# Block products in a graph-network kernel: sums kept in three PSUM banks with a read between the products, and SBUF sums taken off GpSimd

## The chip, the core and the metric

The kernel runs on one core of one Trainium2 chip. The metric is the device time of one execution in microseconds (us). Three executions took 2376.56, 2377.87 and 2381.8 us, so the median is 2377.87 us. In what follows PE is TensorE, DVE is VectorE, ACT is ScalarE, POOL is GpSimd and SP is SyncE.

## What is computed

The input is 128 graphs of 64 nodes with 256 features, and one 64 x 64 adjacency matrix for each. Four layers follow each other, each of them `x = layernorm(x + layer(x, adj))`, all in float32. Cut to what matters:

```python
# layer 0: five steps of a gated recurrent cell
for l in range(5):
    agg = A^T @ (h @ weight[l])
    r = sigmoid(agg @ Wir + h @ Whr + b);  z = sigmoid(agg @ Wiz + h @ Whz + b)
    n = tanh(agg @ Win + bi + r * (h @ Whn + bh))
    h = (1 - z) * n + z * h
# layer 1: (adj @ x) @ W1 -> RMS norm -> silu -> @ W2        (256 -> 1024 -> 256)
# layer 2: log map, adj @ x, exp map, projection onto a ball  (row by row)
# layer 3: attention with exp(e_i + f_j) weighted by adj
```

The five recurrent steps hold most of the work: each one multiplies a 256-feature state and a 256-feature aggregate by six 256 x 256 weight blocks.

## The kernel before

Two graphs fill the 128 partitions, four such pairs make a group of R = 512 columns, and 16 groups (g = 0 to 15) make the batch. `group(g)` (from L611) records all operations of one group as a stream. Nothing is issued while recording: `Flow.either` (L150) keeps, for every operation, the engine or the choice of two engines, an assumed duration, and what it must wait for. `Plan.advance` (L71) then lays the operations of up to four groups (WINDOW) out on the engines, earliest start first, with the rank of each 4 us stretch taken from the string CHOICES. The order so found is fixed on every engine by `Flow.issue`. So a change of one operation, of the rank functions or of CHOICES can move every instruction of the program. The planner also knows that a POOL sum and a DVE operation marked `port` shall not run at the same time; nothing on the chip enforces that order between the two engines.

Three recording helpers matter here. `copied` (L330) and `scaled` (L335) are reads of a PSUM bank that go to ACT or DVE (on DVE with a handicap of 0.4 us, LATER). `summing` (L344) is a sum of two SBUF tiles that goes to DVE or, with a handicap of 1.5 us, to POOL; all such sums have the line L347 in the profile. `dve` and `pool` go to one engine.

Every large matrix product is cut into 2 x 2 blocks and done with seven block products instead of eight, from sums of the inputs (tiles tA, tB, ts, s, made by `summing`) and sums of the weights (made once). With m11, m12, ms1 to ms4 and mn22 for the products and u = m11 + ms2, the four result blocks are

```
m11 + m12      u + ms1 + ms4      u + ms3 + mn22      u + ms3 + ms1
```

- The gates r and z (`gate`, L776, and `plus`, L831): banks p1, pu, pv, pw (shown as p_r, p_u, p_v, p_w). m11 is copied out of p1 (`copied`), then m12 is added to it in the bank and ACT takes the tanh straight from there. The other three blocks are built in SBUF tiles uu and uz by five `plus` sums on DVE, each of which reads one bank of 128 x 512.
- The state's share of n (`state_side`, L795, banks p_hx, p_hy): one copy, one scaled read, two plain sums (L793) and three sums with bias (L807).
- The input's share of n (`input_side`, L843, banks p_ix, p_iy): six sums on DVE (L852), four of 256 columns, one that adds one product to three blocks (768) and one that reads two products at once (512).
- The hidden layer of layer 1 (`by_sums`, L956, banks p_1h, p_uh, p_vh, p_wh): for each of two column halves q, two copies and five sums (L972). Its squares are added up by seven `summing` calls (L949 to L955, tile sqt).
- The way back (`by_sums_back`, L1022, banks p_ox, p_oy): seven sums of 256 columns (L1051) and one of 512 (L1067).

A bank is one unit for the planner and for the semaphores: a product into a bank waits for every earlier read of that bank. In one recurrent step of one group, nine products are recorded behind such a read of their own bank (three in the gates, four in the state's share, two in the input's share).

The last two groups (14 and 15) have `summed` false: their layer norms take their statistics on DVE.

Of the kernel before, what the change touches and what calls it, by code (L numbers as in the profile page):

```python
# [16 lines left out]
P = 128  # L17
# [36 lines left out]
class Plan:  # L54
# [15 lines left out]
    def advance(self, until, rank):  # L70
# [3 lines left out]
        while self.left and clock["PE"] < until:  # L74
            best = None
            for s in range(self.first, min(self.first + flow.WINDOW, len(self.queues))):
                for e, q in self.queues[s].items():
                    opened = False
                    for _, o in zip(range(flow.AHEAD[e]), q):
# [12 lines left out]
                        key = (t + flow.LATER.get((e, len(o.ways) > 1 and o.eng), 0.0), *rank(s, o))  # L92
# [36 lines left out]
class Flow:  # L129
# [16 lines left out]
    LATER = {("DVE", "ACT"): 0.4, ("POOL", "DVE"): 1.5}  # L146
# [6 lines left out]
    WINDOW, STRETCH, LAGS = 4, 4.0, (60.0,)  # L153
    CHOICES = ("0011200000220021202000222000000001000001011000200022110000002002022002112211120201000120000200002022"
               "0200011101200002210100000000222211100211000102210222210000000000211100011010001021111120212101000000"
               "0010210010100101002201011100000000000021002211102210200001020200200202200000012002201221010100002000"
               "0202022000000020022202222010022000002022022002222202220200110100022000000220200020002220011010102100"
               "2200000002202000002001110222000022000000000000022210200012222220120100201112002012121100100100121001"
               "201010010201111111011011000100111011111111111110110111000111011101100001010000100100")
# [81 lines left out]
def kernel(  # L241
# [102 lines left out]
    def summing(n, o, x0, x1, op, w, r):  # L344

        def run(v):
            return lambda: v.tensor_tensor(o(), x0(), x1(), op)  # L347
        flow.either([("DVE", 0.145 + 0.00105 * n, run(nc.vector)), ("POOL", 0.24 + 0.00211 * n, run(nc.gpsimd))], w, r, port=("DVE", "POOL"))
# [264 lines left out]
    def group(g):  # L613
# [128 lines left out]
        def gated(l, h):  # L742
# [49 lines left out]
            def onto(o, ps, j, x, w, r):  # L792
                dve(HR + 44, lambda: nc.vector.tensor_add(o(), ps[:, j * HR:(j + 1) * HR], x()), w, [ps, *r])  # L793

            def state_side():  # L795

                px, py = bank("p_hx"), bank("p_hy")
                su, sv = ((lambda c=c: uz[:, c, half(0)]) for c in range(2))

                def b(c):  # L800
                    return half_b[:, 2 * KD + c:2 * KD + c + 1]

                def out(n, c):
                    return lambda: hnb[:, c, half(n)]

                def biased(n, c, ps, j, x, r):
                    dve(HR + 44, lambda: nc.vector.scalar_tensor_tensor(  # L807
                        out(n, c)(), ps[:, j * HR:(j + 1) * HR], b(c), x(), OP.add, OP.add), [(hnb, (n, c))], [ps, r, half_b])

                prod(px, 0, w_hn, m11, block(0, 0)[1], True)  # L810
                copied(HR, su, lambda: px[:, :HR], [(uz, (0, 0))], [px])
                prod(px, 0, w_hn, m12, block(1, 0)[1])
                scaled(HR, out(0, 0), lambda: px[:, :HR], lambda: 1.0, lambda: b(0), [(hnb, (0, 0))], [px, half_b])
                prod(px, 1, w_hn, ms2, sum_of(t2)[1])
                onto(su, px, 1, su, [(uz, (0, 0))], [(uz, (0, 0))])
                prod(py, 0, w_hn, ms3, sum_of(t3)[1], True)
                onto(sv, py, 0, su, [(uz, (0, 1))], [(uz, (0, 0))])
                prod(py, 1, w_hn, ms1, sum_of(t1)[1])
                prod(py, 0, w_hn, mn22, sum_of(t4)[1])
                biased(0, 1, py, 0, su, (uz, (0, 0)))  # L820
                biased(1, 1, py, 1, sv, (uz, (0, 1)))
                prod(py, 1, w_hn, ms4, block(1, 1)[1])
                biased(1, 0, py, 1, su, (uz, (0, 0)))

            p1, pu, pv, pw = bank("p_r0"), bank("p_u"), bank("p_v"), bank("p_w")
# [5 lines left out]
            def plus(o, n, ps, x, m):  # L831
                dve(R, lambda: nc.vector.tensor_add(o[:, :, half(n)], feats(ps.tile()), x[:, :, half(m)]), of(o, n), [ps, *of(x, m)])  # L832
# [10 lines left out]
            def input_side():  # L843
# [3 lines left out]
                def quarters():  # L847
                    return uu.tile().rearrange("p c (n r) -> p (c n) r", n=2)

                def onto(i, n, src, ps):  # L850
                    w = [(uu, (j % 2, j // 2)) for j in range(i, i + n)]
                    dve(HR * n + 40, lambda: nc.vector.tensor_add(  # L852
                        quarters()[:, i:i + n, :], src(), quarters()[:, i:i + n, :]), w, [ps, *w])

                prod(px, 0, w_in[l], m11, block(0, 0)[0], True)
                prod(px, 1, w_in[l], m12, block(1, 0)[0])
                onto(0, 1, lambda: px[:, :HR].unsqueeze(1), px)
                onto(0, 1, lambda: px[:, HR:2 * HR].unsqueeze(1), px)
                prod(py, 1, w_in[l], ms3, sum_of(t3)[0], True)
                prod(py, 0, w_in[l], ms1, sum_of(t1)[0])  # L860
                onto(3, 1, lambda: py[:, HR:2 * HR].unsqueeze(1), py)
                onto(3, 1, lambda: py[:, :HR].unsqueeze(1), py)
                prod(px, 0, w_in[l], ms2, sum_of(t2)[0])
                onto(1, 3, lambda: over(px[:, :HR], 3), px)
# [356 lines left out]
```

## Time and profile before

One execution was profiled: it took 2377.02 us, of which the span from the first to the last instruction is 2375.1 us.

| | before |
|---|---|
| median of three runs | 2377.87 us |
| profiled execution / its span | 2377.02 / 2375.1 us |
| PE busy, matmul instructions | 2317.0 us (98%), 12754 |
| DVE busy | 1988.6 us (84%) |
| ACT busy | 1272.5 us (54%) |
| POOL busy | 378.6 us (16%) |
| chain that ended last | PE 88%, DVE 9%, ACT 2% |
| DMA | 35.3 MB, mean 15 GB/s |

How to read it: a float32 matmul of 256 columns is two instructions of 128 x 256, each shown as 379 ns long, but they follow each other every 216 ns, since they are pipelined. A short wait of PE is therefore inside its busy time, and waits are better read from the starts of its instructions. PE's weight loads have a row of their own, PEld. An idle time is named with the instruction that ended it. In the groups of instructions, the last number after the bar is the idle time of the engine just before them.

### The profile page before, as it was taken

The numbers are of one execution on the slowest core, as the hardware profiler recorded it, in microseconds if no ns is written. First come the engines' busy times: TensorE is split into PE (matmuls) and PEld (weight loads), VectorE is DVE, ScalarE is ACT, GpSimd is POOL, SyncE is SP. The second block draws the span as 40 slices with busy tenths as digits, with TensorE's granted clock in tenths as the row PEclk, the third lists the DMA queues.
The fourth block names the chain that finished last, engine by engine and source line by source line (L and its number), as shares of the span: only waits on it lengthen the run. The fifth ranks groups of instructions, "written<-read, shape, count | busy, mean of one in ns | idle before, by whom it ended". The sixth has DMA issues, their size and how long they took to land.

```text
span 2375.1 us, 34664 instructions
## 1 busy us (share of the span) xinstructions
PE 2317.0 (98%) x12754; PEld 2056.6 (87%) x12754; DVE 1988.6 (84%) x4305; ACT 1272.5 (54%) x2793; POOL 378.6 (16%) x343
## 2 busy tenths in 40 slices
PE   9999999999999999999999999999999999999985
PEld 7888988898888888888898888988889889888874
DVE  5788888888888888888888888888888888789896
ACT  3344564756555556565555556555555544635475
POOL 3200101110130110112011110202211101001141
PEclk9999999999999999999999999999999999999987
DMA  3000000000000000000000000000000000000000
GB/s 123 10 1 12 1 27 3 27 3 1 29 1 19 12 1 30 1 30 1 27 3 1 30 1 30 1 11 19 1 30 1 27 3 1 19 10 1 18 10 18
DMA packets 40520, 35.29 MB, mean 15 GB/s; under 512 B 9972, under 2 KB 39696, under 8 KB 40352
## 3 DMA queue, kind: packets, MB, share of 16 engines
q1 hardware_dynamic: 38624, 31.20, 4.2%
q8 instruction: 101, 1.65, 0.3%
q10 hardware_dynamic: 1328, 1.31, 0.2%
q0 software_dynamic: 400, 0.57, 0.1%
q14 instruction: 67, 0.55, 0.1%
HBM read 24.69 MB, written 8.39 MB: 14 GB/s over the span
## 4 chain that ended last, share of the span: by engine, by line
PE 88%; DVE 9%; ACT 2%; issue 1%; POOL 1%; POOLq 0%; ACTq 0%; DVEq 0%
PE p_w L782 11%; PE p_v L782 11%; PE p_r L782 11%; PE ps_agg L315 7%; PE p_hy L788 6%; PE p_iy L788 5%; PE p_u L782 5%; PE p_oy L1042 5%; PE p_hx L788 4%; PE p_ix L788 4%; PE p_ox L1042 4%; PE ps_hr L656 3%; PE p_vh L967 2%; PE p_1h L967 2%; PE p_wh L967 2%; PE ps_a L315 2%
## 5 line engine op out<-in xcount | busy, mean ns | idle before, releaser
L712 POOL TENSOR_TENSOR rstd<-ve,pow 128x4 f32<-128x4 f32 (+1 forms) x64 | 77.5, 1212 | 801.2 <-DVE ve L704 761.0
L782 PE MATMUL p_v<-tA,w_h 128*128 128x256 f32 x640 | 170.4, 379 | 0.1
L782 PE MATMUL p_v<-tB,w_a 128*128 128x256 f32 x640 | 169.2, 379 | 0.5 <-DVE tB L347 0.5
L782 PE MATMUL p_r<-hT,w_h 128*128 128x256 f32 x640 | 168.5, 380 | 0.0
L782 PE MATMUL p_r<-agg,w_a 128*128 128x256 f32 x640 | 166.6, 379 | 0.7 <-ACT agg L333 0.7
L333 ACT COPY agg<-ps_agg 128x512 f32<-128x512 f32 x156 | 91.1, 584 | 121.8 <-PE ps_agg L315 121.1
L835 ACT ACTIVATE U<-U,half_b 128x512 f32<-128x512 f32 (+1 forms) x160 | 94.1, 629 | 108.1 <-DVE U L832 108.0
L315 PEld LDWEIGHTS ps_agg<-edge,hr 128*128 128x128 f32 x1024 | 137.3, 191 | 7.5 <-ACT hr L333 0.2
L315 PE MATMUL ps_agg<-edge,hr 128*128 128x128 f32 x1024 | 139.0, 275 | 0.0
L788 PE MATMUL p_hy<-tA,w_hn 128*128 128x256 f32 x480 | 132.8, 381 | 3.6 <-DVE V L793 2.3
L788 PE MATMUL p_iy<-tB,w_in 128*128 128x256 f32 x480 | 133.4, 380 | 1.4 <-DVE V L852 1.4
L782 PEld LDWEIGHTS p_v<-tB,w_a 128*128 128x128 f32 x640 | 120.2, 190 | 16.5 <-DVE tB L347 0.9
L782 PEld LDWEIGHTS p_r<-agg,w_a 128*128 128x128 f32 x640 | 119.6, 190 | 16.4 <-ACT agg L333 1.1
L782 PEld LDWEIGHTS p_v<-tA,w_h 128*128 128x128 f32 x640 | 119.2, 190 | 15.9 <-DVE V L832 0.5
L835 ACT ACTIVATE V<-V,half_b 128x256 f32<-128x256 f32 (+1 forms) x160 | 87.5, 586 | 79.8 <-DVE V L832 79.7
L782 PEld LDWEIGHTS p_r<-hT,w_h 128*128 128x128 f32 x640 | 115.4, 190 | 13.1 <-issue 0.5
L333 ACT COPY hr<-ps_hr 128x512 f32<-128x512 f32 x117 | 68.2, 585 | 103.5 <-PE ps_hr L656 94.8
L899 ACT ACTIVATE V<-V,cols 128x512 f32<-128x512 f32 x96 | 64.7, 715 | 104.0 <-DVE V L852 103.9
L338 ACT ACTIVATE x_n<-y,off,rstd 128x256 f32<-128x256 f32 x175 | 92.3, 589 | 46.3 <-DVE off L716 46.2
L701 ACT ACTIVATE x_n<-y,mv 128x256 f32<-128x256 f32 x168 | 83.3, 498 | 57.0 <-DVE mv L699 57.0
L656 PE MATMUL ps_hr<-ident,hT 128*128 128x128 f32 x640 | 101.4, 273 | 6.8 <-DVE hT L907 6.5
L656 PEld LDWEIGHTS ps_hr<-ident,hT 128*128 128x128 f32 x640 | 79.7, 141 | 25.9 <-issue 9.9
(292 smaller groups left out, 6327.8 us busy)
## 6 DMA issues: line engine op xcount, KB each, us to landing
x<-in_x_dram SPq DMA_DIRECT2D x16, 512.0 KB, 3.9
xr<-in_x_dram SPq DMA_DIRECT2D x16, 512.0 KB, 3.9
out_dram<-x_n SPq DMA_DIRECT2D x16, 512.0 KB, 2.9
edge<-in_adj_dram SPq DMA_DIRECT2D x32, 64.0 KB, 2.3
wm<-in_L_gnn_weight_dram SPq DMA_DIRECT2D x5, 256.0 KB, 5.1
w2f<-in_L_gnn_W_dram SPq DMA_DIRECT2D x4, 256.0 KB, 6.2
w_in_L_gnn_w_hh_dram<-in_L_gnn_w_hh_dram ACTq DMA_DIRECT2D x1, 512.0 KB, 5.3
w_in_L_gnn_w_ih_dram<-in_L_gnn_w_ih_dram ACTq DMA_DIRECT2D x1, 512.0 KB, 6.7
```

The lines of the kernel that those rows point to most:

```text
L315: return nc.tensor.matmul(o, lhsT, rhs, start=(k == 0), stop=(k == nk - 1))
L333: flow.either([("ACT", 0.22 + 0.00077 * n, lambda: nc.scalar.copy(o(), i())), ("DVE", 0.145 + 0.00105 * n, lambda: nc.vector.tensor_copy(o ...
L338: flow.either([("ACT", 0.3 + 0.0008 * n, lambda: nc.scalar.activation(o(), i(), AF.Identity, bias=bias(), scale=scale())), ("DVE", 0.145 + ...
L656: turn(lambda j=j, c=c: nc.tensor.transpose(ps[:, j * D + c * P:j * D + (c + 1) * P], src[:, c, (HB * n + j) * P:(HB * n + j + 1) * P], id ...
L701: act(400, lambda b=b: nc.scalar.activation(o[:, b, :], y[:, b, :], AF.Square, bias=mv[:, b, 0:1], accum_out=st[:, b, 1:2]), [(o, b), (st, ...
L712: pool(1.25, lambda: nc.gpsimd.tensor_tensor(rstd[:, :m, :], ve[:, :m, :], pow2[:, :m, :NB], OP.pow), [rstd], [ve])
L782: pe(HR, lambda i=i, w=w, c=c: nc.tensor.matmul(ps[:, c * HR:(c + 1) * HR], w[:, m, c * P:(c + 1) * P], v[i][0](), start=first and i == 1 ...
L788: pe(HR, lambda: nc.tensor.matmul(ps[:, j * HR:(j + 1) * HR], w[:, m, :], v[0](), start=first, stop=True, skip_group_check=True), [ps], [( ...
L835: act(HR if len(w) == 1 else R, lambda: nc.scalar.activation(o(), src(), AF.Tanh, bias=half_b[:, i * KD + c:i * KD + c + 1], scale=0.5), w ...
L899: act(R, lambda c=c: nc.scalar.activation(uu[:, c, :], uu[:, c, :], AF.Tanh, bias=bih(2 * KD + c)), [*of(uu, 0, c), *of(uu, 1, c)], [*of(u ...
L967: pe(HR, lambda c=c: nc.tensor.matmul(ps[:, c * HR:(c + 1) * HR], w1f[:, w, (2 * q + c) * P:(2 * q + c + 1) * P], v[0](), start=first and ...
L1042: pe(128, lambda j=j, k=k: nc.tensor.matmul(ps[:, i * HR + j * P:i * HR + (j + 1) * P], val(v[k // 2])[:, k % 2, j * P:(j + 1) * P], w2f[: ...
```

## The change

The seven products are gathered in three banks, and the sums that share u are taken from one bank that keeps growing. For the gates, bank pa receives m11, ms2, ms1 and ms4 one after the other and is read after each; pb receives m12; pc receives ms3 and then mn22. The first reads of a block become copies (`taken`, ACT or DVE) and only the second reads are sums on DVE. The last read of pa is ACT's tanh itself.

```diff
+            gate(pa, m11, block(0, 0), True, True)
+            taken(uu, 0, pa)
+            gate(pb, m12, block(1, 0), True, True)
+            plus(uu, 0, pb)
+            tanh_r(0)
...
-            gate(pu, ms2, sum_of(t2), True, True)
-            plus(uu, 1, pu, uu, 1)
-            gate(pv, ms3, sum_of(t3), True, False)
-            plus(uz, 1, pv, uu, 1)
-            gate(pw, ms1, sum_of(t1), True, False)
-            gate(pv, mn22, sum_of(t4), False, True)
-            plus(uz, 1, pw, uz, 1)
-            plus(uz, 0, pv, uu, 1)
-            gate(pw, ms4, block(1, 1), False, True)
-            plus(uu, 1, pw, uu, 1)
+            gate(pa, ms2, sum_of(t2), False, True)
+            taken(uz, 0, pa)
+            gate(pc, ms3, sum_of(t3), True, True)
+            taken(uz, 1, pc)
+            gate(pa, ms1, sum_of(t1), False, True)
+            plus(uz, 1, pa)
+            gate(pc, mn22, sum_of(t4), False, True)
+            plus(uz, 0, pc)
+            gate(pa, ms4, block(1, 1), False, True)
+            tanh_r(1, pa)
```

`state_side` follows the same pattern in regions of two banks: four reads with bias (`begun`, a `scaled`, ACT or DVE) and three sums (`added`) in place of a copy, a scaled read, two sums and three sums with bias. Behind a read of their own bank stand now four products in the gates, five in the state's share and five in the input's share.

```diff
+                def begun(n, c, ps, j):
+                    b = half_b[:, 2 * KD + c:2 * KD + c + 1]
+                    scaled(HR, lambda: hnb[:, c, half(n)], lambda: region(ps, j), lambda: 1.0, lambda: b, [(hnb, (n, c))], [ps, half_b])
+                def added(n, c, ps, j):
+                    dve(HR + 44, lambda: nc.vector.tensor_add(hnb[:, c, half(n)], region(ps, j), hnb[:, c, half(n)]),
...
                 prod(px, 0, w_in[l], m11, block(0, 0)[0], True)
+                prod(py, 0, w_in[l], m12, block(1, 0)[0], True)
+                onto(0, 0, px, 0)
+                prod(py, 1, w_in[l], ms3, sum_of(t3)[0])
+                onto(0, 0, py, 0)
                 prod(px, 0, w_in[l], ms2, sum_of(t2)[0])
+                onto(1, 1, py, 1)
+                onto(0, 1, px, 0)
                 prod(py, 1, w_in[l], mn22, sum_of(t4)[0])
+                prod(px, 0, w_in[l], ms1, sum_of(t1)[0])
+                onto(0, 1, py, 1)
+                onto(1, 1, px, 0)
+                prod(px, 0, w_in[l], ms4, block(1, 1)[0])
+                onto(1, 0, px, 0)
```

`input_side` (above) has seven sums of 256 columns in place of the six wider and narrower ones. `by_sums` has four copies and three sums for each half in place of two and five, and `by_sums_back` seven sums of 256 columns with the 512-column one gone.

The sums of SBUF tiles no longer have a choice of engines:

```diff
     def summing(n, o, x0, x1, op, w, r):
-
-        def run(v):
-            return lambda: v.tensor_tensor(o(), x0(), x1(), op)
-        flow.either([("DVE", 0.145 + 0.00105 * n, run(nc.vector)), ("POOL", 0.24 + 0.00211 * n, run(nc.gpsimd))], w, r, port=("DVE", "POOL"))
+        dve(n, lambda: nc.vector.tensor_tensor(o(), x0(), x1(), op), w, r, True)
+
+    def pool_sum(n, o, x0, x1, op, w, r):
+        pool(0.24 + 0.00211 * n, lambda: nc.gpsimd.tensor_tensor(o(), x0(), x1(), op), w, r)
```

`pool_sum` is used for x1 + b2 (tile xb, 128 x 1024) in all groups, and for the sums of squares (sqt, 128 x 512) and x3 + W_b (x_n, 128 x 1024) in groups 0 to 13. All other SBUF sums are DVE's.

The planner's order is written anew: LATER becomes SOONER (a handicap of 0.4 us for the DVE way of any operation with two ways), LAGS grows from one value to three (30, 90 and 150), which gives CHOICES the digits 0 to 4, and the string CHOICES is another one.

## The prediction, made before the changed kernel ran

> **What bounds the kernel now.** I read the page's busy shares first, then busy time by 100 us stretches, then who PE waits for.
>
> ```profile
> span 2375.1 us, 34664 instructions
> PE 2317.0 (98%) x12754; PEld 2056.6 (87%) x12754; DVE 1988.6 (84%) x4305; ACT 1272.5 (54%) x2793; POOL 378.6 (16%) x343
> ```
>
> ```profile
> 1000.00:1100.00 100.00, 98.51 (x549) 87.35 (x548) 86.82 (x194) 60.81 (x132) 15.21 (x13) 1.00 0.06 18
> ...
> 2200.00:2300.00 100.00, 88.58 (x484) 76.54 (x482) 86.13 (x194) 56.50 (x121) 27.23 (x21) 0.96 0.04 12
> 2300.00:2375.00 75.00, 50.08 (x301) 43.63 (x300) 53.25 (x189) 41.72 (x95) 19.39 (x15) 0.80 0.06 22
> ```
>
> The columns are stretch, length, then PE, PEld, DVE, ACT and POOL busy, then the granted clock. PE is full at clock 1.00 until 2200; the last 175 us are a tail with holes and a lower clock.
>
> Busy time hides short PE waits, so I made a ledger from the starts of its instructions. At the median step of each size (216 ns at 256 columns, 111 at 128, and so on) the 12754 matmuls need 2286.6 us. Before the first lie 2.5 us and behind the last start 11.5. The remaining 74.7 are stalls: 33.5 before 2200 (25.1 in 36 stalls over 0.15 us, 9.6 in stalls of 0.02 to 0.15, the rest rounding) and 41.2 in the tail. The change has the same matmuls, 6922 by the program's count in both orders; only the stalls can change.
>
> What makes the stalls? PE's waits name DVE mostly:
>
> ```profile
> PE ps_sup L315 <- ACT tan L1110: 10.8, 3, 9.5
> PE ps_hr L656 <- DVE hT L907: 6.5, 8, 1.3
> PE ps_T L646 <- ACT x_n L338: 5.4, 3, 2.6
> ```
>
> and the timeline shows what is behind the second line, DVE first, then POOL, then PE (start, duration, what):
>
> ```profile
> 1323.58 0.69 DVE L907 SCALAR_TENSOR_TENSOR hT<-hT,V 128x512 f32<-128x512 f32 x1
> 1324.19 1.76 DVE L347 TENSOR_TENSOR hT<-hT,V 128x512 f32<-128x512 f32 x1
> 1325.98 1.10 DVE L905 SCALAR_TENSOR_TENSOR hT<-U,hT 128x512 f32<-128x512 f32 x1
> 1327.11 1.10 DVE L907 SCALAR_TENSOR_TENSOR hT<-hT,V 128x512 f32<-128x512 f32 x1
> ```
>
> ```profile
> 1323.85 1.55 POOL L347 TENSOR_TENSOR tA<-hT 128x512 f32<-128x512 f32 x1 [5.76 <-DMA out_dram<-x_n]
> 1325.48 1.06 POOL L347 TENSOR_TENSOR tA<-hT,tA 128x256 f32<-128x256 f32 x1
> 1326.61 1.05 POOL L347 TENSOR_TENSOR tA<-tA,hT 128x256 f32<-128x256 f32 x1
> ```
>
> ```profile
> 1328.36 0.63 PE L656 MATMUL ps_hr<-ident,hT 128*128 128x128 f32 x4 [0.98 <-DVE hT L907]
> ```
>
> A DVE operation on SBUF tiles takes 0.69 us alone; beside a POOL sum it takes 1.76, 1.10 and 1.10, and PE then idles 0.98 us. I counted such cases over the trace: 80 DVE instructions are over 0.12 us longer than the median of their kind, all 80 beside a POOL sum, together 54.0 us (46.3 between 100 and 2200, 6.2 in the tail). Of the 37 PE stalls over 0.15 us before 2230, 35 (25.4 of 25.8 us) start within 10 us after one. DVE sums that read PSUM aren't lengthened (0.687 beside POOL, 0.691 alone).
>
> **The change, part by part.** DVE, with durations from these rows:
>
> ```profile
> L852 DVE TENSOR_TENSOR V<-p_ix,V 128x768 f32<-128x768 f32 x48 | 45.9, 957 | 6.9 <-PE p_ix L788 3.6
> ...
> L807 DVE SCALAR_TENSOR_TENSOR hnb<-p_hy,half_b,V 128x256 f32<-128x256 f32 x96 | 43.6, 478 | 16.1 <-PE p_hy L788 15.7
> ...
> L338 ACT ACTIVATE hnb<-p_hx,half_b 128x256 f32<-128x256 f32 x73 | 34.8, 477 | 6.7 <-PE p_hx L788 6.7
> ```
>
> (name, shape and count, then busy us and mean ns, then the idle time ahead). The others come from the same list. 80 recurrent steps (16 groups x 5) each lose two gate sums (0.688) = -110.1 us. The state's share loses three biased sums (0.478) and gains a plain one (0.421) = -81.0. The input's share gains three of 256 and loses the 768 and the 512 (0.957, 0.687) = -30.5. The hidden layer loses 64 x 0.688 = -44.0, the way back 16 x 0.680 = -10.9. Placement in the new order gives DVE 33 more biased reads (0.481) = +15.9, 55 net more copies = +39.6, 41 scalings moved from ACT (25 x 0.407, 16 x 0.345) = +15.7, and in SBUF sums +67 of 256, +43 of 2x256, -17 of 512, -26 of 1024 = +14.5. Sum -191: DVE goes from 84% to about 76%. ACT gains 172 copies (0.583) and 207 biased reads (0.477), loses 74 small copies (0.373), nine of 512, the scalings and three table loads: +141 us, to 59%. None of this is on the path by itself: PE sets the end before 2200, and the sums lie beside it. What counts is how it moves stalls.
>
> *Collisions with POOL.* Before, POOL's SBUF sums take 234.9 us in 195 instructions. After, 98 sums of squares at 1.29 and 30 of 1024 at 2.48 take 201 us: fewer and longer, but not gone. They belong to layers 1 and 3. The lengthening they cause is bounded by two rows: sums of those layers in the trace (59 instructions, 84 us) lie beside 12.9 us of lengthening, 0.154 per us, hence 31 us; the few of exactly these tiles gave 0.33 each for squares (6) and 0.88 each for the 1024 (4), hence 59. I take 31, since ten instructions are few, plus 2 for the weight sums at the start, against 54 before. Per us of lengthening PE lost 25.1/46.3 = 0.54. So 21 x 0.54 = -11 us; the upper bound gives +4.
>
> *New waits of PE.* Each step has 14 products behind a read of their own bank, before 9. A waiting product holds PE's whole queue, all groups. I measured in the program order how much PE work (216 ns per instruction) stands between the product that is read and the one that waits, less the read's duration and 0.37 us for both handovers (0.15 back to PE, as 1328.21 to 1328.36 above; 0.22 to the read, of which 0.16 is the part of a matmul's 379 ns beyond its 216 ns step). Under 0.5 us to spare: 32 on DVE reads before, 240 after; on ACT reads 191 and 332. Price: below, nothing (of the stalls over 0.15 us before 2230 only 0.35 us lies away from a collision, with 223 such waits in place); above, the 9.6 us of small stalls spread over those 223, 43 ns each, times 349 = 15 us. I take +3. But tight waits also let a late DVE through to PE more often. DVE's idle share grows from 16 to 24%, so a delay of 1 us is made up in 4 us instead of 6; the DVE waits under 1 us triple (147 to 443). So 0.54 may become 0.7: 33 x 0.16 = +5.
>
> The Trainium skill (TensorE: Matmul & The Clock Gate, "A second HAM failure mode: psum-queue depth-cycling") speaks against this change: PE that cycles through PSUM banks idles in small bits between groups of matmuls, and its clock swings between half and full. Here the nine waits per step left the clock at 1.00 in every stretch before 2200, through stalls up to 1.6 us; only after the 2.9 us hole before p_vh at 2266.90 did eight matmuls take some 0.43 us each instead of 0.216, 1.8 us lost. By the rule, one such drop in each of 80 steps would be +144 us; by the row, 0. I take 0, since it needs holes of about 3 us, where the planner has four groups to fill from.
>
> *Tail.* Behind the last product of the recurrent steps the new order has 73.4 us of PE work by its steps (before 76.7), 247 DVE operations (261), and one POOL sum where before there were 16. On DVE, groups 14 and 15 lose eight PSUM sums of 0.688 and two of 0.680 there and get 14 SBUF sums of 0.688, about +3 us, and group 13 leaves 16 operations in place of 37. The 6.2 us of lengthening there lie mostly in the chain that ended last (2247.9 to 2249.9, 2260.5). Against it, 3.3 us of PE work move ahead of the tail. I take -6 + 3 = -3, between -9 and +3.
>
> Sum: -11 + 3 + 5 - 3 = -6 us on the profiled 2377.0; the median stands 0.9 above that. I forecast -8, as the lower load of DVE and the copies on ACT (which no collision lengthened) are counted at nothing above, where they can only help: 2370.
>
> **Rivals.** 0.2% of the time is 4.8 us, about what a measurement of this kernel can tell from no change.
> - *Collisions merely change place* (chance 0.22). The upper bound: 59 + 2 us of lengthening in place of 54 gives +4, tight waits +3, tail -6: about 2378. For it: POOL's sums lose only 14% of their time. Against it: the sums of the recurrent steps (hT, tA, tB), which lie beside about three quarters of the lengthening, are gone.
> - *PE pays for DVE's delays through its own banks* (chance 0.18; slower). Place: products into p_ga, p_ix, p_hx behind a DVE read. Price: 61 us of lengthening at 0.8 = 49 us of stalls in place of 25, +24, small stalls +3, tail -3: 2402 at the far end, 2390 in the middle of the case. For it: the tight DVE reads grow from 32 to 240. Against it: reads of PSUM are not themselves lengthened. It decides once over 30 us reach PE, 0.75 of 40 us or 0.55 of 55.
> - *The stalls before 2200 nearly vanish* (0.10, part of faster): no DVE delay reaches PE, -25, tail -3: about 2350.
>
> **Chances and range.** Faster by over 0.2%: 0.60 (0.50 for the sum above, with its own range 2358 to 2373, and 0.10 for the last rival). Within 0.2%: 0.22. Slower: 0.18. The range leaves out about one in ten on each side: 2352 (into the last rival) to 2390 (the middle of the slower case).
>
> **What would show it.** DVE near 1800 us and ACT near 1410; PE's matmuls at 2286.6 by its steps. Right: lengthened DVE instructions sum to some 33 us, stalls before 2200 fall to about 30, none longer than 2 us, clock 1.00. Wrong: PE waits on p_ga, p_ix or p_hx led by DVE reads (the second rival), or lengthening beside sqt and x_n as large as before (the first). The tail from the last p_ix or p_iy to the end takes 129.7 us now; over 132 would break that step.

## The result and the profile after

The changed kernel takes 2356.59 us (median of 4 runs, 2354.67 to 2358.43), the kernel before in the same session 2378.9 us (2376.56 to 2381.8). The ratio is 0.9906 with a 95% interval of 0.9888 to 0.9923: 22.3 us or 0.94% faster, where 8 us were forecast. The profiled execution took 2354.67 us, its span is 2352.9.

The page of the changed kernel, its span and the busy time of each engine:

```profile
span 2352.9 us, 34518 instructions
...
PE 2305.2 (98%) x12754; PEld 2052.8 (87%) x12754; DVE 1811.5 (77%) x4183; ACT 1401.5 (60%) x3043; POOL 346.0 (15%) x276
```

DVE and ACT are where the sum put them (about 1800 and 1410 us), and the matmuls are the same 12754. The stretches of 100 us, with the columns as before (start and end, length, PE, PEld, DVE, ACT, POOL, clock):

```profile
1000.00:1100.00 100.00, 100.00 (x545) 89.61 (x544) 76.81 (x175) 67.01 (x143) 19.45 (x14) 1.00 0.06 18
...
2200.00:2300.00 100.00, 92.51 (x546) 81.78 (x545) 89.57 (x194) 55.56 (x106) 14.50 (x9) 0.98 0.05 17
2300.00:2353.00 53.00, 24.40 (x117) 19.48 (x116) 33.30 (x143) 27.39 (x68) 7.64 (x7) 0.75 0.06 20
```

PE is full at clock 1.00 in the middle again, and every stretch before 2200 has 1.00. The tail is shorter, not denser. Whom PE waits for in the whole execution (who waits, for what, us in total, times, the longest):

```profile
PE ps_T L646 <- ACT x_n L338: 10.1, 2, 10.0
PE ps_sup L315 <- ACT tan L1106: 5.8, 1, 5.8
...
PE p_ah L967 <- ACT hid L333: 2.4, 3, 2.0
...
PE p_ix L788 <- DVE U L848: 1.8, 1, 1.8
...
PE p_gc L782 <- DVE y L679: 1.3, 1, 1.3
...
PE p_ga L782 <- DVE agg L334: 1.1, 1, 1.1
PE ps_hr L656 <- DVE hT L907: 0.7, 1, 0.7
```

The first two are the tail. Before it, ps_hr for hT has gone from 6.5 us in 8 waits to 0.7 in one. What the change adds is products behind a read of their own bank, and yet the waits for such reads by DVE have shrunk in the recurrent steps. In before they were led by

```profile
PE p_hy L788 <- DVE V L793: 2.3, 3, 1.0
PE p_hy L788 <- DVE hnb L807: 2.0, 3, 1.4
PE p_ix L788 <- DVE V L852: 1.7, 3, 1.2
```

and with p_iy (1.4), the other plain sums of p_hy (1.3) and one more wait of p_ix (0.2) they made 8.9 us in 14 waits. In after they are 2.9 us in three: p_ix with 1.8 and 0.5, and p_gc with 0.6 for its copy into U. The rows of p_gc and p_ga above are of other kinds: p_ga waits for its operand agg, and p_gc for the read (into y) of the tile that its bank held before.

The ledger from the starts of the matmuls, made as before. The last product of the recurrent steps divides body and tail:

| us | before | after |
|---|---|---|
| matmuls at their median steps | 2286.6 | 2286.6 |
| before the first | 2.5 | 2.5 |
| stalls until the last recurrent product | 34.2 | 17.8 |
| of these over 0.15 us (number) | 25.7 (37) | 12.5 (20) |
| of these 0.02 to 0.15 us | 9.7 | 6.8 |
| stalls behind it | 40.5 | 34.0 |
| last start to the end | 11.5 | 12.3 |

The two rows "of these" add up to more than the row above them, since steps a little shorter than the median count as negative stalls; the last matmul's step of 0.2 us is in the first and in the last row.

So the body gave 16.4 us and the tail 6.5, against +0.7 at the very end. What is surprising is how the body gave them. The lengthening of DVE instructions beside POOL, which was to fall, did not: between 100 and 2200 us it was 46.3 us in 67 instructions, and is 45.6 in 48 (one of them, 0.4 us, not beside POOL). The sums of squares cause most of it now (a row of POOL's groups, one of those of sqt: name, shape, count, then busy us and mean ns of one):

```profile
L348 POOL TENSOR_TENSOR sqt<-sqt,sqh 128x512 f32<-128x512 f32 x56 | 73.5, 1313 | 160.5 <-ACT sqh L953 152.7 <-DVE hid L334 4.9
```

In this stretch the sums of squares lengthen 35 DVE instructions by 28.8 us, those of xb six by 9.7 and those of x_n six by 6.8. But PE hardly notices. Here is such a place in the timeline of after, first POOL, then DVE, then PE (start, duration, what, the idle time before it):

```profile
2057.70 1.27 POOL L348 TENSOR_TENSOR sqt<-sqt 128x512 f32<-128x512 f32 x1 [3.75 <-ACT sqt L953]
2059.05 1.59 POOL L348 TENSOR_TENSOR sqt<-sqt,sqh 128x512 f32<-128x512 f32 x1
```

```profile
2055.90 0.69 DVE L972 TENSOR_TENSOR hid<-p_ah,hid 128x512 f32<-128x512 f32 x1
2056.78 0.42 DVE L848 TENSOR_TENSOR U<-p_ix,U 128x256 f32<-128x256 f32 x1 [0.20 <-PE p_ix L788]
2057.12 0.68 DVE L345 TENSOR_TENSOR tB<-agg 128x512 f32<-128x512 f32 x1
2057.72 1.80 DVE L905 SCALAR_TENSOR_TENSOR hT<-U,hT 128x512 f32<-128x512 f32 x1
2059.55 1.64 DVE L907 SCALAR_TENSOR_TENSOR hT<-hT,V 128x512 f32<-128x512 f32 x1
2061.23 0.69 DVE L345 TENSOR_TENSOR tA<-hT 128x512 f32<-128x512 f32 x1
```

```profile
2059.61 1.05 PE L315 MATMUL ps_agg<-edge,hr 128*128 128x128 f32 x8
2060.50 0.60 PE L782 MATMUL p_ga<-hT,w_h 128*128 128x256 f32 x2
2060.93 1.03 PE L782 MATMUL p_gb<-hT,w_h 128*128 128x256 f32 x4
2061.80 1.03 PE L782 MATMUL p_ga<-agg,w_a 128*128 128x256 f32 x4
```

The two DVE instructions take 1.80 and 1.64 us instead of 0.69, 2.1 us late in all, and PE shows no idle time: what it does meanwhile doesn't ask for them.

### The profile page after: what moved, and what is told of

Read it like the earlier page. It is cut to its first block, busy times and chain, and to the rows that moved or that the text cites. A ratio compares the mean times of both kernels' runs of the same rounds, so it can differ in the third digit from the quotient of the medians.

```text
span 2352.9 us, 34518 instructions
## 1 busy us (share of the span) xinstructions
PE 2305.2 (98%) x12754; PEld 2052.8 (87%) x12754; DVE 1811.5 (77%) x4183; ACT 1401.5 (60%) x3043; POOL 346.0 (15%) x276
## 4 chain that ended last, share of the span: by engine, by line
PE 91%; DVE 6%; ACT 1%; issue 0%; DMA 0%; POOL 0%; POOLq 0%; ACTq 0%; DVEq 0%
PE p_ga L782 23%; PE p_gc L782 11%; PE ps_agg L315 7%; PE p_hx L788 6%; PE p_gb L782 6%; PE p_ix L788 6%; PE p_ox L1042 4%; PE p_hy L788 4%; PE p_iy L788 4%; PE p_ah L967 4%; PE p_oy L1042 3%; PE ps_hr L656 3%; PE ps_a L315 2%; PE p_ch L967 2%; PE ps_T L646 1%; PE ps_sup L315 1%
## 5 line engine op out<-in xcount | busy, mean ns | idle before, releaser
L782 PE MATMUL p_ga<-tA,w_h 128*128 128x256 f32 x640 | 175.5, 380 | 0.4 <-ACT V L333 0.4
L782 PE MATMUL p_gc<-tA,w_h 128*128 128x256 f32 x640 | 170.9, 380 | 1.9 <-DVE y L679 1.3
L782 PE MATMUL p_gc<-tB,w_a 128*128 128x256 f32 x640 | 171.8, 379 | 0.1
L782 PE MATMUL p_ga<-tB,w_a 128*128 128x256 f32 x640 | 168.4, 379 | 0.0
L782 PE MATMUL p_ga<-hT,w_h 128*128 128x256 f32 x640 | 168.3, 380 | 0.0
L782 PE MATMUL p_ga<-agg,w_a 128*128 128x256 f32 x640 | 167.2, 379 | 1.1 <-DVE agg L334 1.1
L315 PEld LDWEIGHTS ps_agg<-edge,hr 128*128 128x128 f32 x1024 | 145.3, 191 | 10.1
L782 PEld LDWEIGHTS p_ga<-agg,w_a 128*128 128x128 f32 x640 | 120.3, 190 | 17.6 <-DVE agg L334 1.5
L782 PEld LDWEIGHTS p_ga<-tB,w_a 128*128 128x128 f32 x640 | 119.5, 190 | 16.8 <-issue 1.1
L782 PEld LDWEIGHTS p_gc<-tB,w_a 128*128 128x128 f32 x640 | 119.8, 190 | 16.2 <-DVE tB L345 0.5
L782 PEld LDWEIGHTS p_gc<-tA,w_h 128*128 128x128 f32 x640 | 117.8, 190 | 16.7 <-DVE y L679 1.7
```

The costliest lines, as they stand in the source:

```text
L315: return nc.tensor.matmul(o, lhsT, rhs, start=(k == 0), stop=(k == nk - 1))
L782: pe(HR, lambda i=i, w=w, c=c: nc.tensor.matmul(ps[:, c * HR:(c + 1) * HR], w[:, m, c * P:(c + 1) * P], v[i][0](), start=first and i == 1 ...
```

## How the stalls were followed

"Within 10 us after a lengthened instruction", as the prediction counted, says little about a cause, so I followed each stall back. From the matmul that waits I go to the instruction that released it last (by its semaphore), from there to whichever ended later, that instruction's own last releaser or the instruction before it on its engine, and so on until the walk meets PE again, or for at most 12 us. A stall is put down to a collision if a DVE instruction on this walk is over 0.12 us longer than the median of its kind. The same walk from the waits of PE that cost nothing is the control: in before it meets a lengthened instruction in 169 of 1752 of them (10%), against 32 of the 35 stalls over 0.15 us.

| 100 to 2200 us | before | after |
|---|---|---|
| DVE instructions lengthened, us | 67, 46.3 | 48, 45.6 |
| PE waits with one of them on the walk, of all led by DVE or ACT | 207 of 1799 | 83 of 1980 |
| of these, stalls over 0.15 us | 32 (15%) | 12 (14%) |
| their us | 23.5 | 8.1 |
| other stalls over 0.15 us | 1.4 | 3.1 |
| us of stall per us of lengthening | 0.51 | 0.18 |

15.4 of the body's 16.4 us are in the fourth row. A part of the fall from 0.51 to 0.18 is only that the lengthening comes in fewer and longer pieces (0.69 us each before, 0.95 after): by piece, PE loses 0.35 us before and 0.17 after. How far the walk goes is a choice. Cut at 6 to 12 us, and with the semaphore value that each instruction waits for taken from the program, before comes to 0.51 or 0.52 and after to 0.18 to 0.22. Why the pass-through, the us of stall per us of lengthening, fell is the question of the experiments: **A**, POOL's sums (hT, tA, tB before) stood in the chain of the recurrent steps, and those of after do not; **B**, DVE has more idle time (23 instead of 16%) and makes a delay up before PE asks; **C**, it is the order of the products and of their reads itself.

All experiments keep the planned order of one of the two kernels and change an operation only where the order is issued, so that nothing is planned anew. In every table below the lengthening and the stalls over 0.15 us are those from 100 to 2200 us.

## Experiments: where the SBUF sums stand

**The order of before, all 195 SBUF sums of POOL on DVE.**

```diff
         for eng, o in plan.order:
+            if eng == "POOL" and "DVE" in o.ways:
+                eng = "DVE"
             made = o.ways[eng][1]()
```

> The order of before, with the 195 SBUF sums that stood on POOL emitted on DVE at the place where they stood; PE's, ACT's and the other DVE instructions keep their order. DVE should be near 1988.6 - 54 (lengthening) + 119 (124 sums of 512 at 0.688, 67 of 256 at 0.42, 4 of 1024 at 1.39) = 2054 us, 87%. Theory A (what separates before and after is POOL's sums standing in the recurrent chain, where PE waits for their result and for the DVE work that they lengthen): stalls until the last recurrent product fall from 34 to 10 to 18, the time to about 2355. Theory B (DVE's idle share decides how much of a delay reaches PE): with 87% of DVE busy the stalls stay at 30 or more, time 2372 to 2390. Theory C (it is the new order of the products, with other banks): stalls stay within 5 of 34, time near 2375.

2402.72 us (2401.27 to 2404.14), ratio 1.0101 (1.0087 to 1.0115). There is no collision left, and it is 24 us slower. The stalls before the last recurrent product rise from 34.2 to 52.6, none behind a lengthened instruction. PE waits for the moved sums themselves:

```profile
PE p_v L784 <- DVE tB L349: 7.0, 17, 0.8
...
PE p_u L784 <- DVE tB L349: 4.8, 8, 1.4
```

No theory had this size. It shows that collisions were not simply a loss: POOL did this work beside DVE, and in this order DVE has no place for it.

**The order of after, its 128 sums on DVE.** At the same place in the code, a `pool_sum` is emitted with nc.vector.

```diff
+            run = o.ways[eng][1]
+            if hasattr(run, "on_dve"):
+                eng, run = "DVE", run.on_dve
```

> The order of after, with its 128 SBUF sums on POOL (98 of squares, 30 of 1024 elements) emitted on DVE at the place where they stood; nothing else is moved. DVE near 1811.5 - 49 + 98 x 0.688 + 30 x 1.39 = 1871 us, 79%. If collisions still cost PE something in the new order (0.25 of 46 us of lengthening, 10 us of stalls near a lengthened instruction), the stalls before the last recurrent product fall from 17.8 to about 8 and the time to 2347. If these sums lie off PE's chain and their lengthening costs nothing: 2356, within 2. Theory B: DVE's lower idle share gives some back, 2352 to 2362.

2362.03 us (2358.51 to 2362.15), ratio 0.9926 (0.9912 to 0.9940), so 5.4 us slower than after's own median in its session (the intervals of the two ratios overlap a little). The 8.1 us of stalls behind lengthened instructions are gone, but the stalls over 0.15 us are 12.0 in place of 11.2, the small ones until the last recurrent product 10.7 in place of 6.8 and the tail's 37.1 in place of 34.0. So what the collisions still cost in after is at most what the same sums cost on DVE. This version doesn't beat after.

**The order of after, before's 136 recurrent sums on POOL**, once without after's own 128 sums on POOL and once with them.

```diff
-                summing(R, lambda v=v: hN[:, :, v], lambda v=v: h[:, :, v], lambda v=v: uu[:, :, v], OP.subtract,
+                resumming(R, lambda v=v: hN[:, :, v], lambda v=v: h[:, :, v], lambda v=v: uu[:, :, v], OP.subtract,
...
+            if hasattr(run, "on_pool"):
+                eng, run = "POOL", run.on_pool
```

> The order of after, but POOL has the sums that before had on it in the recurrent steps, the same 136 (39 and 36 and 29 of the three kinds of block sums, 32 of the differences of h and the candidate) in the same groups and steps, and none of after's own 128 (these are on DVE). POOL's sums are those of before in place and number, and DVE has near 1871 - 136 sums (103 of them 512 wide at 0.688 is too many: 71 of 512 and 65 of 256, 76 us) = 1795 us plus lengthening. Theory A: the lengthening and the late results stand in the chain again, stalls before the last recurrent product go from 17.8 to 30 or more, time 2368 to 2380. Theory B: DVE's idle share is still 22%, so the stalls stay under 20, time 2355 to 2360. Theory C: under 20 as well.

> The order of after with its own 128 sums on POOL as they are, and the same 136 recurrent sums as in the run before it on POOL as well; POOL near 346 + 165 us, DVE near 1811.5 - 76 = 1736 us, 73%, plus the lengthening of twice as many collisions. Theory A: stalls before the last recurrent product over 35, time 2375 to 2390. Theory B: DVE's idle share is the largest of all, a delay is made up at once: stalls under 20, time near 2356.

2380.06 us (2377.01 to 2381.45), ratio 1.0001 (0.9993 to 1.0010), and 2379.43 us (2378.06 to 2380.23), ratio 1.0002 (0.9994 to 1.0010). In time this is about what theory A expected (2368 to 2380 and 2375 to 2390): these sums on POOL take back the whole gain. Theories B and C missed it: they wanted under 20 us of stalls before the last recurrent product, and there are 40.6 and 38.8. The walk says otherwise about the pass-through:

| | DVE busy | lengthened, us | stalls over 0.15 | behind a lengthened one | per us |
|---|---|---|---|---|---|
| before | 84% | 67, 46.3 | 24.9 | 23.5 | 0.51 |
| after | 77% | 48, 45.6 | 11.2 | 8.1 | 0.18 |
| recurrent sums on POOL, own on DVE | 77% | 58, 41.0 | 23.8 | 9.1 | 0.22 |
| both on POOL | 75% | 100, 83.6 | 25.2 | 17.3 | 0.21 |

With the same sums on POOL as in before, a us of lengthening costs PE 0.22, not 0.51. Theory A is wrong for the pass-through. The traces also show that in before itself PE never waited for the results of these sums: of the stalls over 0.15 us between 100 and 2200, none has one of POOL's hT, tA or tB on its walk, while in the order of after, with both on POOL, 13 stalls with 8.1 us have one. Against after, the last row has 21.0 us more of stalls until the last recurrent product (38.8): twice the collisions (+9.2), other stalls over 0.15 us (+4.8) and small ones (+5.6, 6.8 to 12.4) make up 19.6 of them.

**The order of before, only the 32 differences of hT on DVE.**

```diff
+                flow.ops[-1].ways["POOL"][1].on_dve = True
...
+            if eng == "POOL" and hasattr(o.ways[eng][1], "on_dve"):
+                eng = "DVE"
```

> Before, with only the 32 differences of h and the candidate taken from POOL to DVE at their place; they were beside 24.0 of the 54 us of lengthening. DVE's load stays at 84% (+22 us of sums, -24 of lengthening). Theory A: these stand in the chain to the next step, so the waits of the row products (8.4 us in 10 stalls) and some products vanish, -8 to -12, time near 2368. Theory B: with the load unchanged the remaining 30 us of lengthening give 0.54 each, -24 x 0.54 = -13, less what the sums delay in DVE's queue: 2365 to 2378. If the plan's order alone counts, as where all 195 sums moved cost +24: above 2378.

2375.58 us (2373.49 to 2378.98, 21 runs), ratio 0.9987 (0.9981 to 0.9994): 2 us faster, less than theory A wanted (near 2368) and at the slow end of theory B's 2365 to 2378. The lengthening fell to 31.5 us, the stalls behind it only from 23.5 to 17.2 (0.55 per us), and stalls without a lengthened instruction rose from 1.4 to 6.6. The row products, which were to lose their waits, still wait 7.1 us for hT in 8 waits.

## Experiments: DVE's idle time

**After, DVE filled** with a reduction over 512 constants behind every 14th DVE instruction; the same without collisions; and half as much.

```diff
+                if eng == "DVE":
+                    seen += 1
+                    if seen > 100 and seen % 14 == 0:
+                        last[eng] = self.filler()
...
+    flow.filler = lambda: nc.vector.tensor_reduce(warm[:, :1], w1f.tile()[:, 0, :512], mybir.AxisListType.X, OP.add)
```

> After, with one extra DVE instruction behind every 14th DVE instruction: a reduction over 512 constant elements to one column, whose result nobody reads, about 290 times some 0.6 us, so that DVE is near 84% busy as before, with POOL's sums and the order of everything else as in after. Theory B (DVE's idle share decides how much of a lengthening reaches PE: 0.54 us per us at 84%, 0.25 at 77%): stalls over 0.15 us before the last recurrent product go from 12.5 to 25 or more, nearly all within 10 us after a lengthened instruction, time 2368 to 2378. Theory A (POOL's sums stand off the recurrent chain now): the stalls rise only by what the extra instructions delay by themselves, as much as in the next run, time 2357 to 2364.

> The second run (after's order, its 128 sums on DVE, no collisions) with the same filling: DVE near 1854 + 175 = 2030 us, 86%. It is the base for the run before it: without lengthened instructions, what a DVE of 86% costs by waiting alone. Theory B holds if this run stays near 2362 to 2368 and below the run before it. Theory A: it rises as much as that run or more, since DVE is even fuller: 2366 or more, above that run.

> After, with the extra reduction behind every 28th DVE instruction, half as many as in the run with every 14th (about 139 of 0.677 us, 94 us of instructions, some 70 us of busy time): DVE near 1880 us, 80%. A price that is linear in DVE's load gives half of that run's +43: 2378. A price that sets in above some 80% gives less: 2362 to 2370.

2399.26 us (ratio 1.0087, 1.0073 to 1.0101), 2406.54 (1.0117, 1.0104 to 1.0131) and 2377.19 (0.9992, 0.9985 to 0.9998): +43 us for the full filling, +21 for half, so the price is about linear. Neither theory had this size (2368 to 2378 and 2357 to 2364 for the full filling). The full filling is 278 instructions of 0.677 us, and yet DVE's row says only

```profile
PE 2330.8 (97%) x12754; PEld 2052.3 (86%) x12754; DVE 1946.3 (81%) x4461; ACT 1402.6 (59%) x3043; POOL 347.0 (14%) x276
```

134.8 us more than in after for 188.2 us of filling, since consecutive DVE instructions overlap a little in the records. The lengthening stayed (42.5 and 45.3 us), and the stalls behind it rose from 8.1 to 17.1 (full) and 11.5 (half): 0.40 and 0.25 per us. That is theory B's direction. But theory B also wanted the run without collisions to be the faster one, and it is 7 us slower (36.9 us of stalls, none behind a lengthened instruction), as theory A had it. The filling costs mostly by itself.

**After, the gate copies back on DVE**: real work in place of the filling, and the part of the change that relieves DVE undone.

```diff
                 copied(R, lambda: o[:, :, half(n)], lambda: feats(ps.tile()), of(o, n), [ps])
+                flow.ops[-1].ways["ACT"][1].on_dve = True
...
+            if hasattr(o.ways[eng][1], "on_dve"):
+                eng = "DVE"
```

> After, with the copies of the gate banks (three per step, 214 of the 240 stood on ACT) emitted on DVE at their place: DVE near 1811 + 214 x 0.69 = 1958 us less some overlap, 81 to 83%, ACT near 1401 - 214 x 0.58 = 1277, 54%, both as before; POOL's sums and the order stay those of after. It undoes the part of the change that moves work from DVE to ACT. Theory B: stalls before the last recurrent product go from 17.8 to 40 or more, time 2380 to 2395, like the run with the extra reductions (49.8, 2399). Theory A: under 25, 2357 to 2362.

2391.93 us (2388.82 to 2394.15), ratio 1.0057 (1.0044 to 1.0070), as theory B expected (2380 to 2395). PE waits at the banks of the gates now:

```profile
PE p_gc L784 <- DVE U L336: 4.4, 3, 3.6
PE p_ga L784 <- DVE U L336: 2.8, 2, 1.8
```

In the whole stretch before 2230, the stalls over 0.15 us behind a DVE read of the product's own bank are 22.6 us in 31 here, against 4.4 us in 5 in after and 12.4 us in 18 in before. The longest of them, in PE's timeline:

```profile
933.89 2.08 PE L784 MATMUL p_gc<-tA,w_h 128*128 128x256 f32 x4 [3.56 <-DVE U L336]
```

**After, all optional reads of DVE on ACT.** The opposite direction.

```diff
+            if eng == "DVE" and "ACT" in o.ways:
+                eng = "ACT"
```

> After, with all reads that may stand on DVE or ACT and stood on DVE (86 of 512 elements, 89 of 256, 24 small) emitted on ACT at their place: DVE near 1811 - 100 = 1711 us, 73%, ACT near 1401 + 110 = 1511, 64%. Theory B, taken further: each us off DVE is still worth 0.1 us (the 42 us between after and its run with the sums on DVE gave 5): -5 to -10, 2347 to 2352, faster than both kernels. If ACT's queue takes DVE's place as the late one: stalls led by ACT, 2360 to 2375.

2394.22 us (2391.16 to 2394.65), ratio 1.0067 (1.0054 to 1.0080): 38 us slower than after, on the side that I gave to ACT's queue, and more than I gave it.

```profile
PE 2330.6 (97%) x12754; PEld 2053.2 (86%) x12754; DVE 1709.4 (71%) x3984; ACT 1484.5 (62%) x3242; POOL 345.5 (14%) x276
```

```profile
PE p_ga L784 <- ACT V L335: 3.1, 3, 1.7
PE p_hx L790 <- ACT hnb L340: 3.0, 8, 0.6
```

DVE is at 71%, lower than anywhere, ACT is far from full at 62%, and PE is worse off: before 2230, stalls behind an ACT read of the product's own bank go from 1.2 us in 3 to 15.0 in 26, and 23.4 of the 32.7 us of stalls have no lengthened instruction behind them. Theory B in its simple form, that each us off DVE is worth something, falls here. The pass-through is 0.22 and doesn't fall below that of after either.

**Before, DVE relieved** by doing sums over half of their columns (the other half is left out), and the same with all SBUF sums on DVE.

```diff
-                        quarters()[:, i:i + n, :], src(), quarters()[:, i:i + n, :]), w, [ps, *w])
+                        quarters()[:, i:i + n, :HR // 2], src()[:, :, :HR // 2], quarters()[:, i:i + n, :HR // 2]), w, [ps, *w])
...
+                if o is x and n == m:
+                    part = slice(n * HR, n * HR + HR // 2)
```

> Before, with the PSUM sums that DVE adds in place (the six of the input's share and three gate sums of each step) done over half of their columns; the other half of these sums is left out. The instructions, their order and POOL's sums are those of before; DVE falls by 80 x (2304 x 0.5 + 768) x 1.05 ns = 161 us to about 1828, 77%, the idle share of after. Theory B: stalls over 0.15 us before the last recurrent product fall from 25.7 to about 12, time near 2363. Theory A: they stay at 20 or more, since POOL's sums still stand in the chain, time 2370 to 2376.

> Both of the last readings at once in the order of before: the PSUM sums that DVE adds in place are done over half of their columns (the other half is left out), and all 195 SBUF sums that stood on POOL are emitted on DVE at their place. DVE near 2034 - 161 = 1875 us, 79%. If the gain comes of two things together, recurrent sums off POOL (-18 to -21 in the order of after) and a DVE with room for them, then the stalls before the last recurrent product go from 34 to 20 to 25 and the time to 2360 to 2366. If the new order and its banks do it: above 2368.

2370.14 us (2369.91 to 2372.68), ratio 0.9966 (0.9952 to 0.9979), and 2382.3 us (2379.62 to 2384.31), ratio 1.0013 (1.0006 to 1.0020). The first is 8 us faster than before, half of what theory B expected, and just inside what theory A allowed (2370 to 2376, with 20 us of stalls or more: they are 20.5 until the last recurrent product). With DVE at 78% the lengthening even grew (75 instructions, 53.2 us), and the stalls behind it fell from 23.5 to 18.1 (0.34 per us). The second is not the 2360 to 2366 that relief and no collisions together were to give; it lies where the expectation put the new order as the cause (above 2368). Relief and no collisions together are 12 us slower than the relief alone; PE waits 10.1 us for the moved tB sums (p_v 5.9, p_u 4.2), with DVE at only 79%.

## What the runs say together

| order, change | DVE busy | per us of lengthening | PE waits with a lengthened one on the walk, per lengthened instruction | share of these that stall |
|---|---|---|---|---|
| before | 84% | 0.51 | 207 / 67 = 3.1 | 15% |
| before, differences on DVE | 84% | 0.55 | 131 / 48 = 2.7 | 17% |
| before, DVE relieved | 78% | 0.34 | 180 / 75 = 2.4 | 13% |
| after | 77% | 0.18 | 83 / 48 = 1.7 | 14% |
| after, recurrent sums on POOL | 77% | 0.22 | 96 / 58 = 1.7 | 15% |
| after, both on POOL | 75% | 0.21 | 153 / 100 = 1.5 | 16% |
| after, reads on ACT | 71% | 0.22 | 76 / 47 = 1.6 | 16% |
| after, half filled | 79% | 0.25 | 87 / 50 = 1.7 | 17% |
| after, copies on DVE | 81% | 0.30 | 64 / 49 = 1.3 | 23% |
| after, filled | 81% | 0.40 | 97 / 50 = 1.9 | 26% |

Two things move the pass-through. In the order of after, a late DVE instruction stands behind 1.3 to 1.9 waits of PE in all seven runs, in the order of before behind 2.4 to 3.1 in all three, whichever sums are on POOL and however full DVE is: theory C. And at a fixed order the pass-through follows DVE's load: before falls from 0.51 to 0.34 when DVE is relieved, after rises from 0.18 to 0.40 when it is filled, where more of the waits stall (14 to 17% up to 79% busy, 23 and 26% at 81%): theory B. The relief alone goes about half of the way from 0.51 to 0.18, and what is left falls to the order. Both are in part argued. The relieved run also shortens the instructions that PE waits for. And C is what remains between two orders: no run changed the order of the products and their reads alone, and which property of it counts is not shown. What the traces do show is where the stalls went. Before 2230, those over 0.15 us behind a DVE read of the product's own bank fell from 12.4 to 4.4 us, and those behind an operand that DVE writes from 10.2 to 3.0.

With the walk cut at 6 to 12 us as above, the runs with the copies on DVE, the reads on ACT, half the filling and all of it come to 0.37 to 0.42, 0.19 to 0.33, 0.25 to 0.31 and 0.27 to 0.46, and the relieved one to 0.35 or 0.36. The waits per late instruction change more (before 1.8 to 3.9, after 1.0 to 2.3), but at each cut all three runs of before's order stand above all seven of after's.

The other finding is that every larger shift or addition of work at a fixed order cost time: on DVE +24, +35, +43 and +21, on ACT +38, on POOL +23 twice. The price depends on the order and on the work: 128 sums moved to DVE in after cost 5 us, 195 in before 24. Each order is good with its own placement of the sums. The gain of 22 us therefore can't be split into so much for the products and so much for the SBUF sums by undoing one at a time. A version with one half of the change and an order planned anew for it would do that; it was not run, and this split stays open.

## Why the prediction was right, and which steps of it were not

- *PE's work, DVE and ACT* (2286.6, 1800, 1410 announced): 2286.6, 1811.5 and 1401.5. Right.
- *Clock*: 1.00 in every stretch before 2200, the longest stall before the last recurrent product 1.9 us. The banks that are read between products did not disturb it in after, so the 0 us that the prediction put on the rule of PSUM cycling held. Its reason, that a drop needs a hole of about 3 us, is borne out in the recurrent steps, but the margin is not wide. With the copies on DVE, p_gc once came 3.7 us late behind the copy of its own bank, and with DVE filled, p_ix once came 3.0 us late: each time the next seven matmuls took about 0.43 us in place of 0.216, while single holes of up to 2.0 us in the recurrent steps of these runs left the clock at 1.00. In after's tail two holes of 2.1 us, 3.1 us apart, were enough for a drop.
- *Collisions, -11*: wrong in its first term. The lengthening was to fall from 54 to 33 us, 31 of it from the sums of layers 1 and 3; these gave 45.3 between 100 and 2200. The value per us (0.154) came from a row in which the planner chose POOL where it fitted. The few rows of exactly these tiles, which I set aside as ten instructions, gave the bound of 59 and were nearer. This is the first rival's mechanism, and its sign of being wrong came true: the collisions changed place. Its time (2378) did not, because of the next term.
- *The pass-through, 0.54 to 0.7, +5*: this is the step that failed, with the wrong sign. It fell to 0.18. The waits did become tighter: by the semaphores, PE starts within 1 us of its release in 1307 of 2024 waits, before 1116 of 1916. But that didn't let more delays through, since fewer waits have a delayed DVE instruction behind them at all, 83 in place of 207. I had counted the distance from a product to its read, and not how many waits a late DVE instruction reaches. What the prediction said of DVE's idle share (a delay made up in 4 us instead of 6) accounts for about half of the fall, by the relieved run (0.34), and I let the other argument win.
- The two errors taken together: 45.6 x 0.18 = 8.1 us in place of 23.5, -15.4, where the prediction had -11 + 5 = -6.
- *New tight waits, +3 in small stalls*: they fell from 9.7 to 6.8 us, -2.9. The lower end, nothing, was the nearer one.
- *Tail, -3*: -6.5 in stalls. Its length fell from 129.9 to 120.8 us, 3.3 of that being PE work moved ahead of it. The waits for x_n and tan hardly changed (19.2 to 18.6 us); the hidden layer's products gave 4.0 (10.6 to 6.6) and ps_a 2.1 (2.9 to 0.8). Lengthening in the tail fell from 6.2 to 1.5 us as forecast, but the runs don't show that this is the cause: the order of before without any collision had 46.4 us of stalls in the tail. Left open.
- *The second rival* (PE pays through its own banks): the waits of the recurrent steps behind DVE reads of the product's own bank fell, from 8.9 to 2.9 us by the rows of waits, where it wanted 24 us of stalls more. With DVE fuller, as in the run with the copies on DVE, it is what happens. *The third* (stalls vanish) came halfway: 34.2 to 17.8 us.

The forecast stood on the right side, by a sum in which a saving that didn't happen stood in for one that wasn't foreseen. So its side was in part luck. The time is 2.8 times as far from before as forecast, and 1.4 us below the 2358 to 2373 that the prediction gave to this sum, though inside its whole range.

## What to carry to other kernels

How much a slow instruction costs the bounding engine is not a constant of the hardware: it was 0.18 to 0.55 us per us here, and here it went with how many of that engine's waits had the instruction on the chain behind them and with the load of the slow engine, not with how near a stall was. An order planned for one placement makes each single-part change look bad, so that undoing one part at a fixed order measures the departure from the plan as much as the part. And removing a collision is only worth what the alternative place of that work leaves of it: in the order of before, 54 us of lengthening were cheaper than 119 us more of DVE sums.

## What the runs showed of the hardware

In a collision, who starts first decides. In the timeline above a POOL sum starts at 2057.70 and ends at 2058.97; the DVE instruction that starts at 2057.72 ends at 2059.52, 0.55 us after it, as if it had started over once POOL was done. The next POOL sum, which starts within this DVE instruction, takes 1.59 us in place of 1.27. Take the DVE instructions of after that touch SBUF tiles alone and lie beside POOL's sums of 512 and 1024 columns. Of the 24 that started ahead of the sum none is lengthened. Of the 67 that started within it 48 are; of the other 19, twelve are reciprocals or statistics of a layer norm (none of those is ever lengthened), and seven came in the last 0.22 us of the sum. The lengthened ones are 0.9 us late in the median and at most 1.1 beside the squares (a POOL sum takes 1.3), and up to 2.1 beside the sums of 1024 (these take 2.5). The Trainium skill (SBUF — State Buffer, "SBUF: two separate sides") describes a lock on a port pair that is held by whichever of the two engines starts first, for a whole instruction, while the other is blocked, and these numbers fit it. Its size was what the sum lacked: even a small instruction of 0.17 us (tile mv, L699) took 1.20 beside a sum of squares and 1.66 beside one of 1024. DVE instructions that read PSUM are untouched: none of 217 beside such POOL sums in after is more than 9 ns over its median.
